# Post-norm transformer megakernel: layer norm scalings, the convolution's product groups and the sign FFN's routing stacks issued in another order

## The chip, the cores and the metric

The kernel runs on one core of one Trainium2 chip, as one program. The metric is the device time of that core in microseconds (us), taken as the median of several runs. The engines meant below are TensorE (PE: matmuls and transposes), VectorE (DVE), ScalarE (ACT), GpSimd (POOL) and SyncE (SP, which issues nearly all DMA transfers from one queue, in order).

## The reference

The input x is 2 batches x 1024 tokens x 1024 features, float32. Eight sublayers follow one another, each as `x = layernorm(x + f(x))`, in which the layer norm has no weights:

```python
x = ln(x + L0_attn(x))   # 8 heads of width 16, softmax over 1024 keys
x = ln(x + L0_ffn(x))    # t = x[:, perm]; 16 blocks 64 -> 256, gelu, -> 64; out[:, argsort(perm)]
x = ln(x + L1_attn(x))   # 3-tap convolution 1024 -> 768 over the tokens, gives q, k, v;
                         # causal attention inside blocks of 128 tokens; two projections
x = ln(x + L1_ffn(x))    # routing = softmax(x @ gate.T)                 (8 experts)
                         # (x * (routing @ in_scale)) @ sign(W).T * (routing @ out_scale) + bias
x = ln(x + L2_attn(x))   # Mamba block: selective scan, 2048 channels, 16 states
x = ln(x + L2_ffn(x))    # x[:, perm] @ dequantized int4 weights
x = ln(x + L3_attn(x))   # one-head attention
x = ln(x + L3_ffn(x))    # dense layer + 8 LoRA experts mixed by a router
```

(Here `L0_attn` has 8 heads over 128 columns, 16 each; its softmax is divided by sqrt(128).) The change touches layer 0, the convolution of `L1_attn` and the start of `L1_ffn`.

## The kernel before

The batches are worked one after the other, batch 1 about 2688 us behind batch 0, with the same code. The residual stream of a batch stays in SBUF twice: `x`, eight tiles of 128 tokens x 1024 features, and `xT`, its transpose, features on the partitions, in eight chunks of 128 features. Half h of a batch is tokens 512h to 512h + 511: tiles 0 to 3 or 4 to 7.

*Layer norm.* After each sublayer a tile goes through four steps. Its result is added into `x` out of PSUM, half a row at a time (`add_x`, L152, DVE), and its statistics are taken (`ln_stats`, DVE). `ln_roots` makes the reciprocal roots of several tiles at once (two small activations on ACT, five small steps on DVE). `ln_scale` (L185 to 187) is one DVE instruction of 128 x 1024 that subtracts the mean and multiplies by the root. `to_xT` (L126 to 135) transposes the tile on PE, eight transposes into two PSUM banks (L130), and copies each bank into `xT`; these copies alternate between DVE (L97) and ACT (L99). `add_y` (L139 to 148) is the first two steps for a tile that arrives transposed: eight transposes of `y` pieces, two additions, statistics.

*Order.* There are two ways. Inside `with self.tc.manual_schedule()` every engine executes its instructions in the order in which the Python text issues them. Outside of it a scheduler chooses. All lines of the change stand inside such blocks, though the code right behind the convolution's block is scheduled. Eight PSUM banks and eight 128 x 1024 weight buffers (`self.w`) go round; a load into a weight buffer waits until its last reader is done.

*Layer 0.* `attend(h)` works a half's attention in 16 steps, `blocks(h)` a half's FFN in eight steps j: `ups` (L424, PE) for the next j, Gelu on ACT, `downs` (PE), a copy `o` on DVE, and a scatter by POOL that undoes the permutation in DRAM (`yd`). `store(h)` writes `xT` of a half to DRAM (SP), `gather` reads it permuted (POOL, `t` pieces), and `back` reads `yd` again (SP, `y` pieces). The layer norm of one half is woven into the steps of another: `line(h, first, n)` builds a table `e` from step to work; `n[0]` to `n[3]` are the steps at which the four tiles get their sum and statistics (`first`), `n[4]` the step of the roots, `n[5:]` the steps of the four tiles' scaling and transposes. It is used three times: for tiles 0 to 3 within `attend(1)`, for tiles 4 to 7 within `blocks(0)`, and for tiles 0 to 3, with the FFN's result, within `blocks(1)`:

```python
e = line(0, project, (0, 1, 3, 4, 5, 6, 7, 8, 9))       # in attend(1)
e = line(1, project, (-1, -1, 0, 0, 1, 1, 2, 2, 3))     # in blocks(0); store(1) at 3
e = line(0, lambda tt: self.add_y(tt, ys), (2, 3, 3, 4, 5, 6, 6, 7, 7))  # in blocks(1)
```

*Layer 1's convolution.* The three taps are computed as a fast FIR scheme: `conv(h, co)` is one group of 128 output columns for a half, 32 matmuls of 256 tokens in four parts j of eight (L606), whose moving data are sums and differences of neighbouring tokens. For half 0 `sums0(j)` makes them on DVE. For half 1 POOL makes them (L573) in place, in `xT` itself and in `u0`, once tiles 4 to 7 are there. `calls(c, j)` issues one part of eight matmuls. `c0`, `c1` and `c2` are the first three groups of half 0. While c0 and c1 run, tiles 4 to 7 are still in layer 0's last layer norm (`add_y` to `to_xT`), and the two are interleaved by hand. In batch 0 the weights' sums are made by DVE (L593 to 595) and kept in DRAM for batch 1, and `l2_dequant`, called once per group from c2 on, unpacks a later sublayer's int4 weights: loads on SP, steps on DVE, scatters by POOL (L1516, L1519).

*Layer 1's sign FFN.* `route(h)` gives three steps: `logits` (PE, then ACT), `softmax` (DVE mostly), and `back`, whose last step writes `rT`, the transposed routing. `stack(out, in_, c)` splits a 32-row table into two parts of lower precision, stacked (one copy on ACT, two steps on DVE, the last at L912). It uses the small table `part`, loaded from DRAM at the start of the stage, and makes `ic` (input scales), `oc` (output scales) and `rT`. `signs(k)` turns one of eight weight chunks (`l_fw`, by SP) into signs on ACT. `scale(h, ks)` multiplies chunks of `xT` by `ic` x `rT` (PE L952, then DVE). `scale_in(tt)` splits a tile of `xT` into two parts `hi` and `lo` (ACT, DVE), `scale_out(tt)` makes the output scales (PE L967, ACT). `product(tt, nh)` is the matmul of a tile and half the columns. `project(tt, nh)`, from the stage before, is the last projection of convolution attention for tiles 4 to 7; its additions into `x` and statistics are DVE's.

Of the kernel before, what the change touches and what calls it, by code (L numbers as in the profile page):

```python
# [27 lines left out]
class Net:  # L28
# [185 lines left out]
    def l0(self, b):  # L214
# [7 lines left out]
        with self.tc.tile_pool(name=self.nm("l0a"), bufs=1) as lp, self.tc.tile_pool(name=self.nm("l0b"), bufs=2) as tp:  # L222
# [249 lines left out]
            def line(th, first, n):  # L472


                t4 = [4 * th + q for q in range(4)]
                e = {}
                for tt, m in zip(t4, n[:4]):
                    e.setdefault(m, []).append(lambda tt=tt: first(tt))
                e.setdefault(n[4], []).append(lambda: self.ln_roots(t4))
                for tt, m in zip(t4, n[5:]):  # L480
                    e.setdefault(m, []).append(lambda tt=tt: (self.ln_scale(tt), self.to_xT(tt)))
                return e

            def at(extra, n, f):
# [3 lines left out]
            with self.tc.manual_schedule():  # L488
                self.table()
                for s in (1, 0):  # L490
                    for _ in qkv(s, 0, False):
                        pass
                for tt in range(4, NT):
                    self.to_xT(tt)
                for _ in qkv(1, 1, False):
                    pass
                side = [f for s, th in ((0, 1), (2, 0), (2, 1)) for f in [qkv(s, th, True)] for _ in range(5 if s else 4)]
                for n, _ in enumerate(maxima(0)):
                    for f in side[:1]:
                        next(f)  # L500
                        del side[0]
                for f in side:
                    next(f)
                for tt in range(4, NT):
                    self.add_row(row, tt)
                m = maxima(1)
                attend(0, {n: [lambda: next(m)] for n in range(16)})
                e = line(0, project, (0, 1, 3, 4, 5, 6, 7, 8, 9))
                at(e, 9, lambda: store(0))
                at(e, 9, lambda: gather(0))  # L510
                attend(1, e)
                project(4)
                project(5)
                e = line(1, project, (-1, -1, 0, 0, 1, 1, 2, 2, 3))
                del e[-1]
                at(e, 3, lambda: store(1))
                for n in (5, 6):
                    at(e, n, lambda: gather(1, 2))
                at(e, 7, lambda: gather(1, 4))
                blocks(0, e)  # L520
                ys = back(0)
                e = line(0, lambda tt: self.add_y(tt, ys), (2, 3, 3, 4, 5, 6, 6, 7, 7))
                blocks(1, e)
# [6 lines left out]
    def l1_attn(self, b, yd, op):  # L530
        nc, i = self.nc, self.i
        row = self.row("l1_projb")
        with self.tc.tile_pool(name=self.nm("l1a"), bufs=1) as lp, self.tc.tile_pool(name=self.nm("l1s"), bufs=2) as spool:
# [105 lines left out]
            with self.tc.manual_schedule():  # L639
                c0[0]()  # L640
                sums0(0)
                sums0(1)
                c1[0]()
                ys = [t for q in range(4) for t in (vh[:, q, :HALF], vh[:, q, HALF:])]
                for k, t in enumerate(ys):
                    nc.sync.dma_start(t, yd[k * P : (k + 1) * P, :])

                def calls(c, j):
                    for f in c[1][8 * j : 8 * j + 8]:
                        f()  # L650

                calls(c0, 0)
                sums0(2)
                calls(c0, 1)
                calls(c0, 2)
                calls(c1, 0)
                self.table()
                self.add_y(4, ys)
                self.add_y(5, ys)
                self.ln_roots([4, 5])  # L660
                self.ln_scale(4)
                self.add_y(6, ys)
                self.to_xT(4)
                self.ln_scale(5)
                sums0(3)
                calls(c1, 1)
                self.to_xT(5)
                calls(c0, 3)
                c0[2]()
                c2 = conv(0, 2)  # L670
                c2[0]()
                self.add_y(7, ys)
                self.ln_roots([6, 7])
                calls(c1, 2)
                self.ln_scale(6)
                self.to_xT(6)
                self.ln_scale(7)
                calls(c1, 3)
                self.to_xT(7)
                c1[2]()  # L680
            for k in range(KD):
                sums(nc.gpsimd, 1, slice(k, k + 1), [(j, moving(1, j, k).unsqueeze(1)) for j in (2, 3, 0, 1)])
            for co in range(2, 6):
# [207 lines left out]
    def l1_ffn(self, b, project, early):  # L891
        nc, i = self.nc, self.i
        row = self.row("l1_fb")
        with self.tc.tile_pool(name=self.nm("l1f"), bufs=1) as lp, self.tc.tile_pool(name=self.nm("l1t"), bufs=2) as tp:
# [89 lines left out]
            with self.tc.manual_schedule():  # L984
                self.table()
                r0, r1 = route(0), route(1)
                r0[0]()
                project(4, 0)
                project(4, 1)
                r0[1]()  # L990
                project(5, 0)
                r0[2]()
                stack(ic, ics, 2)
                for k in range(KD):
                    signs(k)
                project(5, 1)
                scale(0, range(KD))
                stack(oc, ocs, 2)
                scale_in(0)
                scale_out(0)  # L1000
                project(6, 0)
                project(6, 1)
                self.table()
                project(7, 0)
                project(7, 1)
                self.ln_roots([4, 5, 6, 7])
                self.add_row(row, 0)
                for n in range(NT):
# [935 lines left out]
```

## Time and profile before

| | |
|---|---|
| time before, median of 3 runs | 5376.52 us (5371.23 to 5391.84) |
| profiled execution | 5374.18 us, its span 5372.4 us |
| mean granted TensorE clock | 0.964 of full speed |
| busy: PE / DVE / POOL / ACT | 92% / 60% / 38% / 36% of the span |

The stages that the change touches, in the trace of that execution (in us; batch 0 and batch 1):

| stage | length | PE busy | clock |
|---|---|---|---|
| layer 0, `attend(1)` | 58.0; 55 | 52.77; 49.78 | 0.94; 1.00 |
| layer 0, `blocks(0)` | 51.7; 52.4 | 40.83; 40.58 | 0.96; 0.96 |
| layer 0, `blocks(1)` | 53.0; 52.3 | 42.67; 42.16 | 0.94; 0.93 |
| convolution up to c2 | 52.7; 45.9 | 40.44; 38.30 | 0.87; 0.93 |
| convolution, the next groups | 69.7; 55.4 | 58.09; 55.40 | 0.93; 1.00 |
| sign FFN, logits to first product | 35.7; 35.0 | 23.81; 21.63 | 0.76; 0.80 |

The granted clock is the share of its full speed at which TensorE was let run. A row of the timeline reads: start, length, engine, source line, operation, output <- inputs, shape, and in brackets how long the engine had stood idle before it and what released it; so "[1.95 <-DVE x L186]" is 1.95 us of idle PE, ended by the DVE instruction of line 186 that writes `x`. A row of the waits reads: engine, what it wanted to do, what it waited for, then the total, the number of times and the longest. A row of the windows gives a stretch, its length, the busy time of PE, PE's weight loads, DVE, ACT and POOL (with the count of instructions), the granted clock, the DMA share and GB/s.

### The profile page before, as it was taken

How to read it: one execution, taken by the hardware profiler on the slowest of the kernel's cores; microseconds unless marked ns; L12 is line 12 of the kernel's file. 1: busy time of each engine (PE TensorE's matmuls, PEld its weight loads, DVE VectorE, ACT ScalarE, POOL GpSimd, SP SyncE). 2: the span in 40 equal slices, each digit the busy share in tenths (PEclk: the TensorE clock that was granted, in tenths of full speed). 3: DMA queues.
4: the chain of work that ended last, by engine and by line, in shares of the span. 5: the costliest groups of instructions: out<-in, count | busy, mean ns of one | idle time of the engine just before them, and what ended most of it. 6: DMA issues, size and time to landing. Idle time of an engine off the chain costs nothing.

```text
span 5372.4 us, 51914 instructions
## 1 busy us (share of the span) xinstructions
PE 4953.8 (92%) x17608; PEld 2461.5 (46%) x17608; DVE 3202.9 (60%) x4386; ACT 1944.0 (36%) x3935; POOL 2023.6 (38%) x1195
## 2 busy tenths in 40 slices
PE   8879988999999999998998899789999999999988
PEld 3346745444444444454433476454444444444533
DVE  5453256279999997314364422551899999953243
ACT  2421232367756552001024211323677665410110
POOL 1013110077778884100010220200877888821010
PEclk9999989999999999999999999899999999999989
DMA  2145311277787996101121432113877889950100
GB/s 92 40 149 180 100 50 50 97 225 210 209 243 213 262 265 196 63 32 43 47 72 40 145 121 90 53 53 104 243 206 214 244 225 262 262 170 32 63 8 32
DMA packets 263356, 726.00 MB, mean 135 GB/s; under 512 B 37040, under 2 KB 54576, under 8 KB 263092
## 3 DMA queue, kind: packets, MB, share of 16 engines
q1 hardware_dynamic: 256820, 701.70, 43.5%
q0 software_dynamic: 6272, 20.98, 1.1%
q8 instruction: 141, 2.31, 0.2%
q14 instruction: 123, 1.01, 0.1%
HBM read 617.43 MB, written 103.02 MB: 134 GB/s over the span
## 4 chain that ended last, share of the span: by engine, by line
PE 68%; DVE 13%; ACT 4%; DMA 3%; issue 2%; POOL 1%; SPq 0%; DVEq 0%; ACTq 0%; POOLq 0%
PE ps L104 26%; PE ps L1364 7%; PE ps L1254 6%; PE ps L606 5%; PE ps L1283 4%; PE ps L1579 4%; DVE h L1261 4%; PE ps L1403 3%; DVE h L1272 2%; PE ps L130 2%; PE ps L1317 2%; ACT ps L1256 1%; DVE st L163 1%; DMA h<-dxd 1%; DVE x L186 1%
## 5 line engine op out<-in xcount | busy, mean ns | idle before, releaser
L1246 POOL TENSOR_TENSOR h<-h,br 128x1024 f32<-128x1024 f32 x512 | 1204.1, 2373 | 28.6 <-DMA h<-dxd 17.9
L1256 ACT ACTIVATE ps<-ps,l_Alog 128x512 f32<-128x512 f32 x1024 | 669.0, 660 | 686.7 <-PE ps L1254 678.9
L1254 PE MATMUL ps<-hi,rep 128*128 128x512 f32 x1024 | 757.9, 740 | 23.3 <-DVE h L1261 14.9
L1261 DVE TENSOR_TENSOR_SCAN h<-ps,h 128x512 f32<-128x512 f32 x512 | 604.7, 1208 | 159.4 <-ACT ps L1256 159.4
L1261 DVE TENSOR_TENSOR_SCAN h<-ps,hst,h 128x512 f32<-128x512 f32 x512 | 632.5, 1266 | 16.0 <-ACT ps L1256 15.5
L1272 DVE TENSOR_TENSOR h<-h,ps 128x1024 f32<-128x1024 f32 x512 | 610.4, 1192 | 0.0
L104 PE MATMUL ps<-w,xT 128*128 128x512 f32 (+1 forms) x1280 | 520.8, 564 | 0.0
L1364 PE MATMUL ps<-xT,w 128*128 128x512 f32 x1024 | 516.4, 608 | 0.0
L1283 PE MATMUL ps<-h,sel 128*32 128x512 f32 x2048 | 410.1, 615 | 72.6 <-DVE h L1272 72.2
L1565 POOL TENSOR_TENSOR x<-x,row 128x1024 f32<-128x1024 f32 x48 | 112.6, 2345 | 876.7 <-PE ps L130 876.7
L152 DVE TENSOR_TENSOR x<-x,ps 128x512 f32<-128x512 f32 x192 | 128.9, 681 | 526.2 <-PE ps L104 379.2
L1254 PE MATMUL ps<-lo,rep 128*128 128x512 f32 x1024 | 408.8, 399 | 0.0
L104 PEld LDWEIGHTS ps<-w,xT 128*128 128x128 f32 x1280 | 248.0, 195 | 257.1 <-issue 250.2
L1254 PEld LDWEIGHTS ps<-hi,rep 128*128 128x128 f32 x1024 | 196.5, 192 | 350.0 <-issue 239.5
L104 PE MATMUL ps<-xT,w 128*128 128x512 f32 x768 | 336.8, 594 | 0.0
L177 ACT ACTIVATE rs<-mv 128x1 f32<-128x1 f32 (+2 forms) x88 | 17.9, 203 | 767.1 <-DVE mv L171 766.8
L130 PE MATMUL ps<-ident,x 128*128 128x128 f32 x1024 | 152.7, 301 | 148.5 <-DVE x L186 138.4
L1254 PEld LDWEIGHTS ps<-lo,rep 128*128 128x128 f32 x1024 | 196.3, 192 | 200.1 <-issue 195.3
L1212 POOL TENSOR_TENSOR e<-e,one 128x512 f32<-128x512 f32 x64 | 81.6, 1274 | 547.7 <-ACT one L1209 375.8
L1364 PEld LDWEIGHTS ps<-xT,w 128*128 128x128 f32 x1024 | 189.2, 192 | 175.3 <-issue 149.9
L1403 PE MATMUL ps<-w,w 128*128 128x512 f32 x512 | 268.0, 605 | 0.0
L1317 PE MATMUL ps<-xT,w 128*128 128x512 f32 x512 | 266.1, 605 | 2.0 <-DVE h L1261 1.9
(283 smaller groups left out, 7402.2 us busy)
## 6 DMA issues: line engine op xcount, KB each, us to landing
h<-dxd SPq DMA_DIRECT2D x512, 512.0 KB, 6.4
w<-l_in SPq DMA_DIRECT2D x128, 512.0 KB, 5.8
w<-l_out SPq DMA_DIRECT2D x96, 512.0 KB, 5.9
w<-l_conv SPq DMA_DIRECT2D x54, 512.0 KB, 3.5
w<-cvd SPq DMA_DIRECT2D x36, 512.0 KB, 3.2
w<-l_fw SPq DMA_DIRECT2D x32, 512.0 KB, 5.7
xcd<-xo SPq DMA_DIRECT2D x64, 256.0 KB, 2.1
szd<-zo SPq DMA_DIRECT2D x64, 256.0 KB, 3.7
```

The costliest lines, as they stand in the source:

```text
L104: self.nc.tensor.matmul(out, lhsT, rhs, start=j == 0, stop=j == n - 1)
L130: nc.tensor.transpose(p[:, j * P : (j + 1) * P], self.x[:, tt, k * P : (k + 1) * P], self.ident)
L606: nc.tensor.matmul(w["p", j // 2][:, 256 * (j % 2) : 256 * (j % 2) + 256], w["w"][j][:, k * P : (k + 1) * P], moving(th, j, k), start=k == ...
L1246: nc.gpsimd.tensor_tensor(hs[k], hs[k], norms[of(k)[0]][1].unsqueeze(1).to_broadcast([P, 2, HALF]), ALU.mult)
L1254: nc.tensor.matmul(dA[k, m], rep[:, 8 * jj + 4 * m + q, :], hl[u, c][n], start=n == 0, stop=n == 1)
L1256: nc.scalar.activation(dA[k, m], dA[k, m], AF.Exp, scale=A[:, g : g + 1])
L1261: nc.vector.tensor_tensor_scan(hs[k][:, m, :], dA.pop((k, m)), hs[k][:, m, :], hst[:, g : g + 1] if u else 0.0, ALU.mult, ALU.add)
L1272: nc.vector.tensor_tensor(hs[k], hs[k], norms[of(k)[0]][3].unsqueeze(1).to_broadcast([P, 2, HALF]), ALU.mult)
L1283: nc.tensor.matmul(py[u, c][32 * j : 32 * j + 32, :], self.sel[:, q, :], hs[k - 1 + j // 2][:, j % 2, :], start=False, stop=q == 3,)
L1317: nc.tensor.matmul(p, w["w"][:, k * P : (k + 1) * P], self.xcols(k, u0, HALF), start=k == 0, stop=k == KD - 1)
L1364: nc.tensor.matmul(p, w["w"][:, k * P : (k + 1) * P], self.xcols(k, u * HALF, HALF), start=k == 0, stop=k == KD - 1)
L1403: nc.tensor.matmul(p, y[:, cc, t * P : (t + 1) * P], wt[:, cc * HALF : (cc + 1) * HALF], start=c2 == 0 and cc == 0, stop=last,)
```

## The change

Only the order of issue changes.

1. In `line` the scalings of all four tiles are issued with the roots, at step `n[4]`; the steps `n[5:]` hold the transposes only. In `blocks(0)` the roots stay at step 1, and the transposes of tiles 4 to 7 move from steps 1, 2, 2, 3 to 2, 2, 3, 3. The store stays at step 3.
2. In the convolution, both scalings of tiles 4 and 5 follow their roots, and tiles 6 and 7 are added, rooted and scaled together before the last part of c0. The groups of eight matmuls now stand before and between the transposes of tiles 4 and 5, and c1's last part before those of 6 and 7.
3. In the sign FFN, the stack of `ic` follows the logits and the stack of `oc` the softmax. The last projections of tiles 6 and 7 stand between the scalings of `xT`, and `scale_in(0)` and `scale_out(0)` around the last ones.

```diff
@@ -477,8 +477,10 @@
                 for tt, m in zip(t4, n[:4]):
                     e.setdefault(m, []).append(lambda tt=tt: first(tt))
                 e.setdefault(n[4], []).append(lambda: self.ln_roots(t4))
+                for tt in t4:
+                    e[n[4]].append(lambda tt=tt: self.ln_scale(tt))
                 for tt, m in zip(t4, n[5:]):
-                    e.setdefault(m, []).append(lambda tt=tt: (self.ln_scale(tt), self.to_xT(tt)))
+                    e.setdefault(m, []).append(lambda tt=tt: self.to_xT(tt))
                 return e
 
             def at(extra, n, f):
@@ -511,7 +513,7 @@
                 attend(1, e)
                 project(4)
                 project(5)
-                e = line(1, project, (-1, -1, 0, 0, 1, 1, 2, 2, 3))
+                e = line(1, project, (-1, -1, 0, 0, 1, 2, 2, 3, 3))
                 del e[-1]
                 at(e, 3, lambda: store(1))
                 for n in (5, 6):
@@ -659,25 +661,25 @@
                 self.add_y(5, ys)
                 self.ln_roots([4, 5])
                 self.ln_scale(4)
+                self.ln_scale(5)
+                calls(c1, 1)
+                self.to_xT(4)
+                calls(c1, 2)
+                self.to_xT(5)
+                sums0(3)
                 self.add_y(6, ys)
-                self.to_xT(4)
-                self.ln_scale(5)
-                sums0(3)
-                calls(c1, 1)
-                self.to_xT(5)
+                self.add_y(7, ys)
+                self.ln_roots([6, 7])
+                self.ln_scale(6)
+                self.ln_scale(7)
                 calls(c0, 3)
                 c0[2]()
                 c2 = conv(0, 2)
                 c2[0]()
-                self.add_y(7, ys)
-                self.ln_roots([6, 7])
-                calls(c1, 2)
-                self.ln_scale(6)
+                calls(c1, 3)
+                c1[2]()
                 self.to_xT(6)
-                self.ln_scale(7)
-                calls(c1, 3)
                 self.to_xT(7)
-                c1[2]()
             for k in range(KD):
                 sums(nc.gpsimd, 1, slice(k, k + 1), [(j, moving(1, j, k).unsqueeze(1)) for j in (2, 3, 0, 1)])
             for co in range(2, 6):
@@ -985,24 +987,25 @@
                 self.table()
                 r0, r1 = route(0), route(1)
                 r0[0]()
+                stack(ic, ics, 2)
                 project(4, 0)
                 project(4, 1)
                 r0[1]()
+                stack(oc, ocs, 2)
                 project(5, 0)
                 r0[2]()
-                stack(ic, ics, 2)
                 for k in range(KD):
                     signs(k)
                 project(5, 1)
-                scale(0, range(KD))
-                stack(oc, ocs, 2)
+                project(6, 0)
+                scale(0, range(4))
+                project(6, 1)
+                scale(0, range(4, KD))
+                project(7, 0)
                 scale_in(0)
+                self.table()
+                project(7, 1)
                 scale_out(0)
-                project(6, 0)
-                project(6, 1)
-                self.table()
-                project(7, 0)
-                project(7, 1)
                 self.ln_roots([4, 5, 6, 7])
                 self.add_row(row, 0)
                 for n in range(NT):
```

## The prediction

> **What bounds the kernel now.** I read four views: the page's busy shares and the chain that ended last, then PE's waits in the windows of the three edited stages, then the timeline of PE there, and last the windows with the granted clock.
>
> ```profile
> PE 4953.8 (92%) x17608; PEld 2461.5 (46%) x17608; DVE 3202.9 (60%) x4386; ACT 1944.0 (36%) x3935; POOL 2023.6 (38%) x1195
> ...
> PE 68%; DVE 13%; ACT 4%; DMA 3%; issue 2%; POOL 1%; SPq 0%; DVEq 0%; ACTq 0%; POOLq 0%
> ```
>
> TensorE is the bound, and the 13% of DVE in the chain is where PE stands and waits for it. PE's waits, first 250 to 372 us (layer 0's FFN of batch 0), then 364 to 460 (the convolution), then 767 to 812 (sign FFN's start); columns are us in total, times, longest:
>
> ```profile
> PE ps L130 <- DVE x L186: 12.8, 8, 3.1
> ...
> PE ps L606 <- DVE w L594: 11.6, 2, 9.3
> PE ps L130 <- DVE x L186: 11.1, 2, 5.6
> ...
> PE ps L967 <- DVE oc L912: 7.1, 1, 7.1
> PE ps L952 <- DVE ic L912: 2.9, 1, 2.9
> ```
>
> L130 is a transpose of x, L186 the scaling in front of it, L912 the last step of a stack. All three edits aim at waits that are really there. The timeline of PE in batch 1 shows each:
>
> ```profile
> 2901.99 1.06 PE L130 MATMUL ps<-ident,x 128*128 128x128 f32 x8 [1.95 <-DVE x L186]
> ...
> 2951.65 1.21 PE L130 MATMUL ps<-ident,x 128*128 128x128 f32 x8 [3.06 <-DVE x L186]
> 2952.79 3.51 PE L424 MATMUL ps<-t,w 64*128 64x512 f32 x8
> ...
> 3024.38 1.09 PE L130 MATMUL ps<-ident,x 128*128 128x128 f32 x8 [1.54 <-DVE x L186]
> ...
> 3058.53 1.94 PE L130 MATMUL ps<-ident,x 128*128 128x128 f32 x8 [5.62 <-DVE x L186]
> ...
> 3456.43 1.22 PE L967 MATMUL ps<-oc,rT 32*128 32x512 f32 x2 [8.55 <-DVE oc L912]
> ```
>
> **The change, part by part.** It adds and removes no instruction of weight; it moves them. Durations: scaling 0.81 us, 0.73 more for each that follows directly; xT copy 0.69 on DVE, 0.59 on ACT; transposes of a tile 1.0; ups or downs 1.92; a group of eight products (L606) 3.47; eviction into x 0.69, statistics 1.5, roots 1.45.
>
> *Layer 0, attention of the second half.* Tile 2's scaling stands on DVE behind the evictions of the first heads, and PE waits 1.95 us in both batches. Scaled at step 5 it is long done. The price is three scalings (2.2 us) ahead of tile 0's xT copy, which comes 0.5 us later (rs ready 201.6 + 3.0 = 204.6, not 204.07); the exponentials pace PE there, so I take 0, at most 0.5. Gain 1.9.
>
> *Layer 0, first FFN half (batch 1's clock).* PE waits 3.06 + 1.61 + 1.16 + 1.61 = 7.4, and the L424 row takes 3.51 in place of 1.99, because Gelu's table load stood behind the xT copy: 9.0 together. With transposes from j=2 on, PE goes on at 2948.6: ups and downs end at 2952.4, the scalings run 2950.8 to 2953.8 beside them, tiles 4 and 5 follow without a wait, tiles 6 and 7 end at 2960.4 instead of 2969.5. What they delay is the o copy, by 1.4 us; its scatter has slack. The store on SP moves from 2969.8 to 2961.0. Next late is POOL: the gathers start when the store has landed, some 9.5 us on (2970.5), so they stay 8.8 ahead. I take 8.7.
>
> *Layer 0, second FFN half.* Waits 1.54 + 1.16 + 1.54 + 1.16 = 5.4. Scalings end at 3024.2, tile 3's transposes at 3028.9 instead of 3034.4. Next late is the last scatter: o is copied at 3026.9 instead of 3029.6, and the new pool's buffers are free 3.3 us after that scatter's start (3030.6 to 3033.9 today), at 3031.2. The sums that start the convolution move from 3034.8 to 3031.3. Gain 3.5, not 5.4. Layer 0 in all: 14.1 a batch, 28.2.
>
> *Convolution, batch 1.* Between 3050.1 and 3082.1 PE waits 5.62 + 1.94 and runs partly at half clock. New order: tiles 4 and 5's transposes to 3052.1, a group of products to 3055.5, a wait of 3.0 for the unchanged scaling at 3058.4, then transposes, group, transposes to 3063.8, y transposes to 3065.7, two groups to 3072.7. DVE meanwhile: scalings to 3059.1, two copies and u, sums0(3) to 3066.4, tiles 6 and 7 to 3071.8, roots and scalings to 3074.8. PE waits 1.5 and ends at 3075.9. Gain 6.2; PE is full from there to 3137, so it stays.
>
> *Convolution, batch 0.* PE reaches group 2 at 392.9 instead of 402.25, but DVE (w L593 to L595) and the queues take some back. The order of the built program shows on POOL that the first dequant scatter, today ahead of the 32 sums, now comes behind them:
>
> ```profile
> 398.77 0.98 POOL L1516 DMA_INDIRECT wq<-w,idx  x1 [50.88 <-DVE w L1515]
> 402.96 3.30 POOL L573 TENSOR_TENSOR xT<-xT 128x256 f32<-128x256 f32 x4 [3.20 <-DVE xT L97]
> 406.23 1.17 POOL L573 TENSOR_TENSOR u<-xT 128x256 f32<-128x256 f32 x2
> 407.36 17.78 POOL L573 TENSOR_TENSOR xT<-xT 128x256 f32<-128x256 f32 x26
> 425.29 0.98 POOL L1516 DMA_INDIRECT wq<-w,idx  x1 [0.15 <-issue]
> ```
>
> On SP the second l_packed load now waits for that scatter, and the next l_conv loads are queued behind it. The sums can start at 391.5 (ACT's copies) and end near 413.5. Then: scatter lands +3.3, l_packed +3.9, DVE 1.5, l_conv +3.9, L593 and L594 2.5: group 4 starts near 430 to 432, today at 439.3; group 5 near 451, today 457.9. Between 3 and 9 gained; I take 7, from the last.
>
> *Sign FFN.* The in-stack's DVE step now stands at the head of the queue and waits for l_part; behind it are tile 4's evictions, which release the logits' softmax. l_part is issued at 768.10, and DMA is idle from 770.5 on, so it costs no more than that. Then DVE is the bound without a gap: stack to 772.5, evictions and statistics to 775.3, softmax 1.9, out-stack 2.0, eviction 0.7, rT 1.5, three evictions with two statistics 4.9, eight scalings of xT 4.8, eviction 0.7, lo 1.3, eviction and statistics 2.1, roots 1.45, lo 1.3, scaling 0.7: 798.7. Tile 4's transposes follow at 799.1, today at 809.22: 10.1. Signs are covered: the fifth l_fw load waits for the in-stack alone (771 instead of 780.8), the sixth for the out-stack (778), so they end near 789, before hi is wanted. PE's projections (3.5 us a tile) are spread over DVE's 24 us. In batch 1 l_part lands 1.4 us later after the logits: 9.5. Together 19.6.
>
> **The clock.** Rows: the same wait of 1.95 us, in batch 0 and in batch 1.
>
> ```profile
> 211.80:214.30 2.50, 0.63 (x8) 0.39 (x4) 1.70 (x4) 0.00 (x0) 0.00 (x0) 1.00 0.00 0
> ...
> 216.00:218.00 2.00, 2.00 (x8) 1.27 (x7) 0.46 (x1) 2.00 (x5) 0.00 (x0) 0.50 0.00 0
> ...
> 2902.00:2904.00 2.00, 2.00 (x13) 1.67 (x14) 1.34 (x2) 0.91 (x2) 0.00 (x0) 1.00 0.04 8
> ```
>
> The Trainium skill ("TensorE: Matmul & The Clock Gate", part 1, "What's actually happening") halves the clock only after an idle window of about 3.4 us. By that rule the gaps left in the new order (3.1, 1.5, 2.8, 1.9 us a batch) cost nothing. The row disagrees: a 1.95 us wait was followed by some 6 us at 0.50. By the row each gap may bring a spell of 3 to 6 us at half speed, 1.5 to 3 us lost, in half of the cases: up to 12 in all. I take 3, since today's gaps, which go, had such spells too.
>
> **Sum.** 28.2 + 6.2 + 7 + 19.6 - 3 = 58. The profiled execution took 5374.2 (span 5372.4 and 1.8 around it), so 5316; the median of the runs shown, 5376.5, lies 2.3 above it: 5318. A difference of 0.5% (27 us) is about what a measurement of this kernel can tell from no change; it took 5371 to 5392 in three runs.
>
> **Rivals.**
> Half of it lost (12%): gaps re-throttle PE again and again (12) and batch 0's convolution gives nothing (7), layer 0's gathers or y loads land late and keep a third of its gain (9): 58 - 25 = 33, 5344. For: y loads already hold PE at 2997 to 3002. Against: store, gathers and y loads all move together.
> No change (8%): layer 0's transfers keep all 24 us of its two FFN halves, and DVE, which is gapless in sign FFN, keeps half of 20: 58 - 34 - 7 = 17 left, 5360. Against: waits for DMA are 3 us there, those for L186 are 13.
> Slower (4%): SP in batch 0's convolution. Each group from the third on, and the projections behind them, then waits in turn for scatter, l_packed, DVE and l_conv, about 16 us by my sum against 14 of products. The slowest landings in the trace (7.2 for l_conv there, not 3.9) would add 3 to each of four rounds. It turns the result only if a round takes 15 us longer than I reckon, four times 15 = 60: 5380, and past 22 it is over 0.5%, 5405. Nothing in the trace is so slow.
> That the scheduler undoes the order is excluded: the built program has the instructions of PE, DVE and ACT as the text of the change puts them.
>
> **The numbers.** My own case has 76%. The range reaches down to 5300: clock spells gone (3), batch 0's own spell of 6 us at half clock gone too (3), its convolution at 9 (2), layer 0's second FFN half at the full 5.4 (4), and the fastest run, 5 below the median, come to 17. Up it reaches to 5346, past the first rival. Faster by over 0.5% takes my case and most of the first rival: 0.86; within 0.5%: 0.10; slower: 0.04.
>
> **What would show it.** Right: no L130 waits for L186 in layer 0's FFN; first sums of the convolution 14 us earlier in each batch; 46 us from there to group 2 becoming 40 in batch 1; logits to tile 4's transposes 32 us instead of 42. Wrong: PE waits of over 2 us for t, y or l_conv in their place, a first dequant scatter later than 16 us before group 4, or a mean clock below 0.964.

## The result, and the profile after

The changed kernel takes 5320.76 us (median of 4 runs, 5318.64 to 5322.97) against 5373.88 us before (4 runs, 5364.95 to 5391.84): a ratio of 0.9897, 95% interval 0.9871 to 0.9923. The profiled execution took 5320.85 us, with a span of 5318.8 us and a mean granted clock of 0.968.

The page's line of busy shares, as before:

```profile
PE 4939.3 (93%) x17608; PEld 2457.1 (46%) x17608; DVE 3195.9 (60%) x4386; ACT 1943.6 (37%) x3935; POOL 2030.5 (38%) x1195
```

TensorE was busy for 4953.8 us before, in the same 17608 matmuls. 14.5 us of the 53.6 that the span lost are therefore matmuls that ran at a better clock (over the whole span the time at half clock fell from 386 to 341 us), and the rest is idle time.

PE's waits in the three edited stages of batch 0: layer 0's FFN (238 to 322 us), the convolution (322 to 453), sign FFN's start (747 to 792). Columns: us in total, times, longest. From the convolution on, line numbers are two higher than before: L608 is the product that was L606, L575 the sums (L573), L595 to L597 the weights' sums (L593 to L595); behind the sign FFN they are three higher (L1519 was L1516).

```profile
PE ps L393 <- DVE aoT L390: 3.1, 2, 2.4
PE ps L424 <- DVE o L450: 1.5, 1, 1.5
...
PE ps L608 <- DVE w L596: 19.5, 4, 10.7
PE ps L608 <- DVE qh L575: 8.2, 1, 8.2
PE ps L130 <- DVE x L186: 4.6, 2, 3.0
...
PE ps L943 <- DVE r L938: 3.0, 1, 3.0
PE ps L130 <- DVE x L186: 1.6, 1, 1.6
```

Layer 0's waits for L186 are gone (12.8 us before, in the view shown with the prediction), and so are sign FFN's waits for the stacks. The convolution is where the time did not go away. Its waits for the scaling fell from 11.1 us to 4.6, but those for groups' weights rose from 11.6 to 19.5 (the longest, group 4's, was there before with 9.3), and ahead of its first product PE now waits 8.2 us for the first sum (L575), where it waited 1.8.

The stages, from the start of one named instruction to the start of another, in us. In brackets is the time at half clock in the stage, taken from the trace's clock records; it agrees with what the windows view gives as 2 x (1 - granted clock) x length.

| stage | batch 0, before | after | batch 1, before | after |
|---|---|---|---|---|
| second half's attention, to the first `ups` | 65.9 (9.4) | 61.1 (2.5) | 64.9 (6.3) | 61.2 (2.7) |
| `blocks(0)` | 51.7 (4.3) | 42.1 (0.9) | 52.5 (3.9) | 43.0 (0.7) |
| `blocks(1)`, to the first product | 53.0 (6.8) | 48.7 (4.5) | 52.3 (6.8) | 48.6 (9.0) |
| convolution, to the projections | 122.2 (23.9) | 123.5 (22.8) | 101.1 (6.8) | 99.0 (8.1) |
| sign FFN, logits to first product | 35.7 (17.1) | 24.8 (3.4) | 35.1 (13.7) | 24.6 (3.4) |
| sign FFN, first product to last addition | 102.6 (13.7) | 106.6 (20.5) | 102.7 (13.7) | 103.5 (13.7) |

The sum of the gains: layer 0 18.7 and 16.9, convolution -1.3 and 2.1, sign FFN's start 10.9 and 10.5, its products -4.0 and -0.8. That is 53.0 of 53.6; all other stages together give the remaining 0.6, with parts of both signs (the scan of batch 1 alone took some 8 longer, that of batch 0 some 3 less).

### The profile page after: what moved, and what is told of

Same layout as the page of the kernel before. It is cut to its first block, busy times and chain, and to the rows that moved or that the text cites. A ratio compares the mean times of both kernels' runs of the same rounds, so it can differ in the third digit from the quotient of the medians.

```text
span 5318.8 us, 51900 instructions
## 1 busy us (share of the span) xinstructions
PE 4939.3 (93%) x17608; PEld 2457.1 (46%) x17608; DVE 3195.9 (60%) x4386; ACT 1943.6 (37%) x3935; POOL 2030.5 (38%) x1195
## 5 line engine op out<-in xcount | busy, mean ns | idle before, releaser
L1249 POOL TENSOR_TENSOR h<-h,br 128x1024 f32<-128x1024 f32 x512 | 1204.8, 2376 | 24.8 <-DMA h<-dxd 13.3
L1264 DVE TENSOR_TENSOR_SCAN h<-ps,hst,h 128x512 f32<-128x512 f32 x512 | 633.3, 1269 | 14.5 <-ACT ps L1259 14.2
L1118 DVE SCALAR_TENSOR_TENSOR ps<-xp,l_convw,ps 128x512 f32<-128x512 f32 x192 | 144.5, 753 | 185.8 <-ACT ps L1113 181.2
```

What stands on the lines that cost most here:

```text
L1118: nc.vector.scalar_tensor_tensor(p, xp[:, k : k + HALF], cw[:, c, k : k + 1], p, ALU.mult, ALU.add)
L1249: nc.gpsimd.tensor_tensor(hs[k], hs[k], norms[of(k)[0]][1].unsqueeze(1).to_broadcast([P, 2, HALF]), ALU.mult)
L1264: nc.vector.tensor_tensor_scan(hs[k][:, m, :], dA.pop((k, m)), hs[k][:, m, :], hst[:, g : g + 1] if u else 0.0, ALU.mult, ALU.add)
```

## The experiments

Each was timed against the kernel before on the same chip. Where an expectation speaks of "the changed kernel", its time is the 5320.76 above; it was not timed again beside the later versions. The kernel before came out between 5372.95 and 5377.84 in these series, so a difference of less than about 5 us between two versions' medians says little by itself.

**Each part alone.** The first is `line` with its changed call, the second the convolution's block, the third sign FFN's block; the rest of each is the kernel before.

> The kernel before with part 1 alone (scalings behind their roots in line, transposes of tiles 4 to 7 at steps 2, 2, 3, 3). Theory A (the gain is the sum of its stages, each keeping what its own trace shows): layer 0 gained 18.7 us in batch 0 and 16.8 in batch 1 of the changed kernel, so 32 to 36 us faster than before, about 5340. Theory B (layer 0's gain is partly eaten at the handover to the convolution, where the last scatter sets the start, and the changed convolution wins some of it back only together with it): under 28 us, 5347 or more. Theory C (most of the gain is TensorE's clock that happens to fall better): no relation to 35; anything from 10 to 50.

> The kernel before with part 2 alone (the convolution's groups and layer norms of tiles 4 to 7). In the changed kernel this stage, from its first product to the attention projections behind it, went from 122.2 to 123.5 us in batch 0 and from 101.2 to 99.0 in batch 1. Theory A: this part is worth 1 to 4 us in all, within 0.1% of before. Theory B (it lost its gain because layer 0 now ends earlier than its last scatter, so that TensorE stands 8.2 and 4.7 us ahead of the first product and works the first group at half clock, 9.96 and 9.46 us for 7.14): without part 1 the first group is at full clock, batch 1 gains 5 to 6 and batch 0 gains 2 to 7, together 7 to 13 us faster. Where batch 0 gains nothing even so, it is the dequantization's scatters behind the sums on GpSimd.

> The kernel before with part 3 alone (sign FFN's stacks under the logits). Theory A: from logits to the first product 10.5 to 10.9 us a batch less, all of it kept: 21 us faster, about 5353. Theory B (batch 0 of the changed kernel gave 3.9 us back between the first and the last product; the new order brings that back with it): 10.5 + 7 = 17 us, 5357. Theory C: the batch that gave back did so by two half-clock spells that come and go with the phase of the clock's windows, so this run can show 14 to 21.

| part alone | median, us | ratio to before, 95% | gain of its stages in the trace, batch 0 and 1 |
|---|---|---|---|
| layer 0 | 5340.9 (6 runs) | 0.9942, 0.9926 to 0.9957 | 14.9, 13.8 |
| convolution | 5371.5 (14 runs) | 1.0000, 0.9989 to 1.0012 | 2.2, 4.5 |
| sign FFN, to the first product | 5360.1 (20 runs) | 0.9970, 0.9961 to 0.9980 | 10.9, 10.9 |

The ratios give 31, 0 and 16 us, together 47 of the 55 that the ratio of all three gives; the intervals are 5 to 8 us to either side, so the parts are additive as far as these runs can tell. Layer 0 is worth most, and as much as theory A said. (The execution that was profiled for it was the slowest of its six, 5360.9 us at a clock of 0.962, so its stages show rather too little.) Part 3 came out nearer to theory B's 17 us than to A's 21, and by the medians at 13: what it gains at its start it lost in part again behind it, as in batch 1, where the products took 104.9 us with 17.1 us at half clock, against 102.7 with 13.7 before. That fits theory C's mechanism.

Part 2 alone fits theory A by its time: the interval, 6 us to either side of no change, leaves out theory B's 7 to 13. Its trace lies between the two, since the stages gained 6.7 us there and other stages gave some of it back. In batch 1 the first group now runs at full clock (7.14 us, where it takes 9.46 in the changed kernel) and the stage takes 96.6 us; so the handover from layer 0 did eat part of that gain (theory B). In batch 0 it gains 2.2 us only. PE's waits there, in the timeline (a group is a row of `qh` and one of `kh`; these are the first halves of groups 3, 4 and 5):

```profile
407.64 10.01 PE L606 MATMUL ps<-qh,w 128*128 128x256 f32 x32 [3.75 <-DVE w L594]
433.88 8.85 PE L606 MATMUL ps<-qh,w 128*128 128x256 f32 x32 [9.32 <-DVE w L594]
452.81 7.17 PE L606 MATMUL ps<-qh,w 128*128 128x256 f32 x32 [3.17 <-DVE w L594]
```

The wait of 9.3 us for group 4's weights stays even without part 1, as it stood in the kernel before, so layer 0 is not its cause.

**Layer 0 without the shift of the transposes.**

```diff
-                e = line(1, project, (-1, -1, 0, 0, 1, 2, 2, 3, 3))
+                e = line(1, project, (-1, -1, 0, 0, 1, 1, 2, 2, 3))
```

> The changed kernel, but in blocks(0) the transposes of tiles 4 to 7 stay at steps 1, 2, 2, 3, as before; the scalings still follow their roots. Theory A (the scalings' place does it): the transposes of tile 4 wait some 3 to 4 us behind the roots of step 1 again, the other three wait for nothing: 3 to 5 us a batch slower than the changed kernel, 6 to 10 in all. Rival (the shift does most of it, as TensorE has nothing else to do beside the roots at step 1): 12 us or more slower, with the long L424 row (3.51 us) back.

5330.50 us (6 runs, ratio 0.9924, 0.9908 to 0.9941): 10 us slower than the changed kernel. `blocks(0)` takes 49.5 and 48.7 us instead of 42.1 and 43.0, and PE waits there once for L186:

```profile
PE ps L130 <- DVE x L186: 3.1, 1, 3.1
```

The scalings' new place removes three of the four waits. The first one, in front of tile 4, is as long as before, since nothing else stands between the roots and that tile's transposes. In the traces the shift is worth 7.4 and 5.7 us of the 9.6 and 9.5 that `blocks(0)` gained; part of it is the clock, for the wait comes with 8.4 and 4.4 us at half clock. That is more than theory A gave it (3 to 5 a batch), and 13 us together is what the rival had said, though the 10 by the medians is not. The rival's sign, the long L424 row, came back in batch 1:

```profile
2929.53 1.09 PE L130 MATMUL ps<-ident,x 128*128 128x128 f32 x8 [3.06 <-DVE x L186]
2930.56 3.68 PE L424 MATMUL ps<-t,w 64*128 64x512 f32 x8
```

In batch 0 it is 2.57. The row is long by as much of it as runs at half clock (2930.6 to 2934.0 in batch 1; in batch 0 only up to 1.2 us into the row).

**Weights ahead of the dequantization, and the dequantization behind all groups.**

```diff
+            nxt = c2
             for co in range(2, 6):
-                load, cs, last = conv(0, co) if co > 2 else c2
-                if co > 2:
-                    load()
+                load, cs, last = nxt
...
                 last()
+                if co < 5:
+                    nxt = conv(0, co + 1)
+                    nxt[0]()
                 if b == 0:
                     self.l2_dequant(co - 2)
```

> The changed kernel, but in the convolution's loop the next group's weights are asked for ahead of the dequantization of this group, so that on SP no l_conv load is queued behind an l_packed load that waits for a scatter. In the changed kernel groups 2 to 5 of batch 0 wait 1.8, 3.8, 10.7 and 3.2 us for the weights' sums, and group 4 also runs its first half at half clock; first product to projections takes 123.5 us. Theory A (the scatter behind GpSimd's sums holds the SP queue, and that is where batch 0's gain went): the wait of 10.7 falls to 2 or less, the stage to 110 to 114, batch 1 unchanged, 10 to 13 us faster than the changed kernel. Rival (the weights' sums on DVE and the DMA queues are the limit anyway): group 5 or the projections wait for what group 4 saves; the stage stays over 119, less than 4 us.

> The changed kernel, but all four dequantizations of batch 0 are issued behind the convolution's groups instead of one behind each. Theory A: as with the loads ahead, the convolution's stage of batch 0 falls from 123.5 to about 108 to 112 (no scatter, no l_packed ahead of any l_conv); the projections behind it then share SP and DVE with the dequantization, and the attention stage of batch 0 (294.5) grows by 0 to 10. Rival: the groups still wait for their weights' sums, as SP can load a group's 1.5 MB only when the group two before has ended: waits of 2 to 4 us a group stay, stage over 117.

With the loads ahead: 5308.51 us (5 runs, ratio 0.9874, 0.9858 to 0.9890), 12 us faster than the changed kernel. The timeline of PE, batch 0, groups 3 (second half) to 5 and the projections:

```profile
400.97 7.07 PE L608 MATMUL ps<-kh,w 128*128 128x256 f32 x32
408.55 7.14 PE L608 MATMUL ps<-qh,w 128*128 128x256 f32 x32 [0.51 <-DVE w L596]
415.53 7.07 PE L608 MATMUL ps<-kh,w 128*128 128x256 f32 x32
427.65 8.72 PE L608 MATMUL ps<-qh,w 128*128 128x256 f32 x32 [5.05 <-DVE w L596]
436.21 7.07 PE L608 MATMUL ps<-kh,w 128*128 128x256 f32 x32
443.35 1.10 PE L104 MATMUL ps<-qkv,w 128*128 128x512 f32 x2
447.97 2.93 PE L104 MATMUL ps<-qkv,w 128*128 128x512 f32 x3 [3.52 <-DMA w<-l_wq]
```

Group 4's wait of 10.7 us is 0.5, the stage takes 108.2 us instead of 123.5, and 5.3 us of that are lost again in the attention behind it (299.8 for 294.5), which waits for its own weights. Theory A holds: the SP queue, held by an l_packed load that waits for a scatter, was where batch 0's gain went.

With the dequantization behind all groups: 5314.89 us (5 runs, ratio 0.9884, 0.9868 to 0.9899), 6 us faster than the changed kernel. From group 2 to the projections there is no wait for weights at all, yet the stage takes 115.8 us, since PE then stands before the projections:

```profile
PE ps L104 <- DMA w<-l_wq: 14.9, 1, 14.9
```

The expected place was right and the size wrong: the whole dequantization moves in front of the next weights on SP, and 7.7 of the 12 to 15 us are left, of which attention takes another 3.6.

**TensorE kept busy ahead of the first product.**

```diff
+                p = self.ps()
+                for n in range((56, 32)[b]):
+                    nc.tensor.transpose(p[:, P * (n % 4) : P * (n % 4) + P], self.ident, self.ident)
                 calls(c0, 0)
```

> The changed kernel with 56 (batch 0) and 32 (batch 1) transposes of the identity added ahead of the convolution's first product; their results are read by nothing. TensorE stands there today for 8.2 and 4.7 us. Theory A (the clock is granted by how busy TensorE was in the window of 3.4 us before): the first group runs at full clock, 7.1 us instead of 9.96 and 9.46, and everything behind it comes 2.8 and 2.3 us earlier; the added work fits into the wait. 5 us faster in all. Rival (the half clock has another cause, or the added work is too late or too long): the first group still takes over 9 us, or it starts later by what it gains; 0 or slower.

5316.17 us (5 runs, ratio 0.9882, 0.9865 to 0.9899). The timeline of PE at batch 1's first product, L656 being the added transposes:

```profile
2991.39 3.66 PE L656 MATMUL ps<-ident 128*128 128x128 f32 x32
2996.26 7.14 PE L608 MATMUL ps<-qh,w 128*128 128x256 f32 x32 [1.21 <-issue]
```

The first group takes 7.14 us in both batches, and batch 1's stage takes 95.0 us with no time at half clock, 6.1 less than before the change, where the prediction had reckoned 6.2 at full clock. Of the 4.0 us against the changed kernel the first group is 2.3. The rest is not the added work's doing: the wait of 3.05 us ahead of tile 4's transposes is here too, and this time no half clock followed it. No other engine's work was moved, and the sums still come when they came. Batch 0 does not show it in the length of its stage (124.1), as its later groups wait for weights anyway. The 4.6 us by the medians are inside the intervals; the verdict rests on the rows.

**The last scatter's source outside layer 0's pool.** (The indices that it reads move too.)

```diff
+                    if th and j >= KD - 1:
+                        o = self.bp.tile([P, D], F, tag="row", name=self.nm("o"))[:, :HALF]
+                    else:
+                        o = tp.tile([P, HALF], F, tag="o", bufs=3, name=self.nm("o"))
```

> The changed kernel, but the copy that the last scatter of layer 0's FFN reads, and the table of indices, lie in a pool that outlives layer 0, so that the convolution's first sums need not wait until that scatter has landed. Theory A (the handover waits for the last scatter alone, which itself waits for the scatter before it): DVE's first sum comes 6.4 us (batch 0) and 3.0 us (batch 1) earlier, right behind the last copy into xT; TensorE's wait falls to 1.8 us, as in the kernel before, the first group runs at full clock (7.1 us); together 9 to 14 us faster than the changed kernel. Rival (the y pieces for tiles 4 to 7 are next late, since they can be read only when the scatter has landed): the first group comes earlier but TensorE then waits at L144 for vh by the same amount; under 5 us.

5313.07 us (5 runs, 5297.46 to 5321.72; ratio 0.9876, 0.9856 to 0.9895). By its time it lies between the theories, 8 us faster than the changed kernel. Batch 1 does what theory A says: `blocks(1)` to the first product takes 43.4 us instead of 48.6. In batch 0 it takes 46.2 instead of 48.7, and PE then waits at a new place. (In this kernel L612 is the product, L579 the sums, L600 the weights' sums.)

```profile
PE ps L612 <- DVE w L600: 19.9, 4, 11.2
PE ps L130 <- DVE x L186: 4.6, 2, 3.0
PE ps L612 <- DVE kh L579: 4.4, 1, 4.4
PE ps L612 <- DVE cb L563: 1.8, 1, 1.8
```

A sum (kh) stands on DVE behind the weights' sums of group 1. Their third load had fallen behind the row l1_bv on SP, which waits for the very scatter that was to be taken out of the way. The stage grew by 5.0 us. For batch 0 that is the rival's outcome by another road, a weight load and not the y pieces.

**Both, and with more waits filled.** The first mends that load's place. The second adds `self.fill(n)`, n transposes of the identity, ahead of four waiting instructions.

> The changed kernel with the loads ahead of the dequantization and the last scatter's source outside layer 0's pool, and the row l1_bv (which waits for that scatter when it takes the source's place) loaded behind the convolution's first weights, so that the third l_conv load of group 1 is no longer queued behind it on SP. Theory A (two separate waits, so their gains add): the convolution's stage of batch 0 at 108 to 111, layer 0's second FFN half to the first product at 45 to 46 in batch 0 and 43 to 44 in batch 1, attention of batch 0 some 5 longer; 15 to 20 us faster than the changed kernel, 5300 to 5306. Rival (with the first group earlier, the weight loads and the y pieces take it back as they did in batch 0 of the kernel with the last scatter's source alone, whose stage grew by 5): no faster than the kernel with the loads ahead alone, 5308.

> The same with transposes of the identity that nothing reads put into four waits of TensorE: 12 ahead of tile 4's transposes in the convolution (a wait of 3.05 us), 12 ahead of sign FFN's first routing transposes (2.96), 28 ahead of the second half's logits (4.2) and 36 ahead of its first scaling (5.4); some 0.11 us each, so that 1.1 to 1.7 us of each wait are left. Theory A (a wait halves the clock of the next window or two of 3.4 us when it leaves TensorE idle for more than about 1.75 us of a window): the half-clock spells behind these waits go, and with them 13.7 to 20.5 us at half clock per batch in the sign FFN's products become 7 or less; 6 to 12 us faster than the kernel of the run before. Rival (the granted clock follows something slower than one window, or the added work delays the waiting work itself): the spells stay, within 3 us of the run before, or slower.

5307.68 us (4 runs, 5298.67 to 5313.93; ratio 0.9871, 0.9851 to 0.9891) and 5303.15 us (4 runs, 5293.92 to 5303.45; 0.9863, 0.9845 to 0.9881). The first is no faster than the loads ahead alone: in batch 0 convolution and attention take 414.3 us instead of 408.0, as group 5 now waits 8.2 us for its weights, and batch 1's `blocks(1)` to the first product takes 47.0 us with 6.8 at half clock, not 43.4. The gains do not add (the rival). The second shows its effect in sign FFN's products of batch 1; these are two windows, of the kernel without and of the kernel with filled waits (columns: window, length, busy PE, weight loads, DVE, ACT, POOL, granted clock, DMA share, GB/s):

```profile
3399.60:3504.50 104.90, 87.28 (x383) 64.31 (x382) 72.92 (x150) 27.85 (x62) 10.37 (x6) 0.92 0.08 28
...
3392.80:3493.80 101.00, 88.84 (x447) 68.51 (x446) 74.25 (x153) 28.37 (x62) 10.42 (x6) 0.98 0.09 29
```

PE does more work there in less time: the half-clock time falls from 17.1 to 3.4 us (in batch 0 from 17.1 to 6.8) and the stage by 3.9. Between the two kernels' medians lie 4.5 us, less than the expected 6 to 12 and inside the intervals.

**Loads ahead, and waits filled.**

> The changed kernel with the loads ahead of the dequantization, with the waits filled as in the run before, and with 56 and 30 transposes of the identity ahead of the convolution's first product in place of the moved source of the last scatter. The moved source gained 5 us at the handover of batch 0 and lost them in that batch's convolution and attention (408 us with the loads ahead alone, 414 with both), and gained up to 5 in batch 1. Theory A (full clock behind the filled waits is worth what the clock table says, and the weights of batch 0 stay in time): batch 0's convolution and attention at 405 to 408, batch 1's convolution at 94 to 96, the products of the sign FFN at 101 to 103 in both batches; 8 to 12 us faster than with the loads ahead alone: 5296 to 5300. Rival (TensorE's time saved there is waited for again): 5303 or more.

5295.86 us (4 runs, 5289.41 to 5301.60; ratio 0.9852, 0.9832 to 0.9871): 25 us faster than the changed kernel and 13 faster than the loads ahead alone by the medians, and the fastest version that was run. Batch 0's convolution and attention take 403.9 us, batch 1's convolution 96.7, the products 99.5 and 101.1. The profiled execution's clock is 0.975.

## Why the prediction was right, point by point

The forecast was 5318 and the measurement 5320.76. The mechanism was right in layer 0 and sign FFN; that the sum came out within 3 us is luck in part. Two terms were wrong in opposite directions: layer 0 gave 7 us more than forecast and the convolution 12 less. The forecast also started from a median of 5376.5, which a fourth run brought to 5373.9: the gain was 53 us, not 58.

| term | predicted | in the trace |
|---|---|---|
| second half's attention, twice | 3.8 | 8.5 |
| first FFN half, twice | 17.4 | 19.1 |
| second FFN half, twice | 7.0 | 8.0 |
| convolution, batch 1 | 6.2 | 2.1 |
| convolution, batch 0 | 7 | -1.3 |
| sign FFN, logits to tile 4's transposes | 19.6 | 20.2 |
| clock, and what lies behind | -3 | -3.0 (remainder) |

- *Clock.* The last row agrees by chance. The -3 stood for half-clock spells behind the gaps that are left, but in the trace each stage's figure holds its own spells already, and the -3.0 is what the other rows leave of 53.6, mostly the products (-4.8). What the clock did shows in PE's busy time: 14.5 us less for the same matmuls. The term had the wrong sign.
- *Sign FFN.* From logits to tile 4's transposes it takes 31.5 us in batch 0 and 31.6 in batch 1, for 42.0 and 41.4 before: 10.4 and 9.8, forecast 10.1 and 9.5. DVE is the bound there, as the step said: in batch 0, from the landing of l_part (751.8 us) to tile 4's transposes (779.2), it waits 0.8 us in all. The order that reads worst, a step waiting for l_part at the head of the queue, cost next to nothing, since the projection that DVE takes next came out of PE no earlier than about 751.4 (half of a row of 3.70 us that starts at 749.57).
- *Layer 0.* The waits went as listed. The excess of 7.4 us over 28.2 is mostly clock: in the stretch of the second half's attention the time at half clock fell by 6.9 and 3.6 us, worth half of that each. Where it did not fall, the stretch gained what was forecast: in the kernel with the added transposes, batch 0 had 10.2 us at half clock there (9.4 before) and took 63.4 us, 2.5 less than before for a forecast of 1.9. The prediction had booked such spells as a loss and set the ones that go against the ones that come; they should have been counted stage by stage. One reading was wrong too, without harm to the sum: the L424 row of 3.51 us was put down to Gelu's table load. This window of the kernel before lies over it; PE is busy throughout, at half clock:

```profile
2952.49:2955.90 3.41, 3.41 (x11) 1.20 (x9) 0.54 (x1) 2.88 (x4) 0.00 (x0) 0.50 0.00 0
```

  The wait of 3.06 us ahead of the row left PE idle for 2.57 us of the window before this one, so wait and long row went together.
- *The last scatter.* It did set the start of the convolution, as the step for the second FFN half said. What was not seen: o was ready 1.2 us (batch 1) and 4.8 us (batch 0) before its scatter started, since each scatter waits for the one before it to land (figures in the last section). Because layer 0's work now ends well ahead of it, PE stands idle for 8.2 and 4.7 us before the first product and runs the first group at half clock. That makes 2.3 of the 4.1 us that batch 1's convolution fell short of its 6.2; another 1.4 went to the group behind the wait of 3.05 us, which takes 4.98 us instead of 3.62.
- *Convolution, batch 0.* This is the step that failed. Its chain was right: first dequantization scatter, l_packed, DVE, l_conv, sums, group 4. It puts 16.5 to 18.5 us from the end of GpSimd's sums to group 4, and the trace has 18.8 (401.2 to 420.0). (Its terms add up to 15.1; the slack above them covered l_conv, which took 7.3 us from its first issue to the sum that waits for it, not 3.9.) The term that was mis-sized is the sums' own time, taken from the row before as 22 us. They took 26.4:

```profile
374.82 6.94 POOL L575 TENSOR_TENSOR xT<-xT 128x256 f32<-128x256 f32 x9 [45.15 <-ACT xT L99]
...
383.42 17.77 POOL L575 TENSOR_TENSOR xT<-xT 128x256 f32<-128x256 f32 x20
401.34 1.00 POOL L1519 DMA_INDIRECT wq<-w,idx  x1
```

  The sums also started 3.1 us later than reckoned, most of it the 2.8 us of the half-clock first group. Together that is 7.5 us, and the forecast was a gain of 7. Why the sums took longer stands in the last section: the new order puts them beside other steps of DVE. The kernel with the loads ahead tests the queue: without l_conv queued behind that scatter the stage falls by 15.3 us, though the sums take 26.1 there. The share of the 7.5 us is read from rows of a trace; no run changed the sums' time alone.
- *The rivals.* "Half of it lost" named its parts rightly (batch 0's convolution gives nothing, PE slows again behind its gaps) but not their balance, since layer 0 did not lose a third. The rival that ends slower named the right place, the rounds on SP in batch 0; they cost 8 us against the forecast, not 60. "No change" did not come: layer 0's two FFN halves gave 27 us, where that rival had their transfers keep all 24.
- *The signs to look for.* "No L130 waits for L186 in layer 0's FFN" and "32 us instead of 42" came true. The first sums came 18.7 and 16.8 us earlier, counted from the second half's attention, where 14 was said. "46 us becoming 40 in batch 1" did not: it is 45.2, from 47.3, measured from the first sum. Of the signs of a wrong forecast one showed: a wait of over 2 us for l_conv's sums in the old one's place.

## What to carry to other kernels

When a step is moved up, ask which instruction now stands in front of an in-order queue with a wait that used to be satisfied: here it was one scatter behind 32 sums, and by way of SP and DVE it cost a stage its whole gain. Do not take an instruction's duration from a row in which another engine did other work beside it. A gap on TensorE costs its own length and the slow time behind it, so reckon a stage with both, and where a gap can't be removed, work that nothing reads can fill it.

## What the runs showed of the hardware

**The clock is decided window by window.** In the trace's clock records every change of the granted clock lies on one grid, and spells last 3.41 us or a multiple of it. That explains why the same wait of 1.95 us in layer 0 was followed by half clock in batch 0 and not in batch 1. These are windows cut on that grid, of the kernel before, first around the wait of batch 0 (212.4 to 214.4 us), then around that of batch 1 (2900.0 to 2902.0); the second column is the length and the third TensorE's busy time, the clock stands behind the five engines:

```profile
211.58:214.99 3.41, 1.46 (x14) 1.06 (x11) 1.70 (x4) 0.00 (x0) 0.00 (x0) 1.00 0.00 0
214.99:218.41 3.42, 3.42 (x13) 1.96 (x10) 1.41 (x2) 2.56 (x5) 0.00 (x0) 0.50 0.00 0
218.41:221.82 3.41, 3.41 (x15) 1.23 (x14) 0.00 (x0) 0.00 (x0) 0.00 (x0) 0.50 0.00 0
...
2897.88:2901.29 3.41, 2.16 (x15) 0.58 (x12) 1.15 (x4) 1.10 (x3) 0.00 (x0) 1.00 0.00 0
2901.29:2904.70 3.41, 2.71 (x15) 2.02 (x16) 1.97 (x3) 1.61 (x4) 0.00 (x0) 1.00 0.02 5
```

In batch 0 the whole wait fell into one window (1.46 us busy, 1.95 idle); in batch 1 it was split (1.25 and 0.70 idle). Counted over both traces, before and after, of the full-clock windows that left TensorE idle for 2.0 us or more all 109 were followed by a window at half clock; of those with less than 1.5 us idle 7 of 2741 were; in between it was 17 of 61. So a wait of 2 us may be free or may cost 1.7 to 3.4 us more (half of a spell of 3.41 or 6.83), by where it falls on the grid. This bears out the row that the prediction sided with, and it agrees with the added transposes: in both batches the first group behind them ran at full clock. Runs of one kernel lie up to 35 us apart (33 runs of the kernel before: 5358.49 to 5393.01), and the longer ones have the lower clock: the ten at a mean clock of 0.963 or less average 5381.8 us, the ten at 0.966 or more 5366.1. That the grid makes this difference is likely, and was not tested.

**GpSimd's sums slow down beside some of DVE's steps, not all.** One sum of 128 x 256 takes 0.61 us, and up to 1.64 when it meets a DVE instruction that reads two tiles from SBUF, such as the weights' sums or the dequantization's last step (`w<-w,w`, 128 x 1024), which then takes up to 1.52 us itself, and 1.23 without a sum beside it. From the changed kernel, batch 0:

```profile
390.78 1.23 DVE L595 TENSOR_TENSOR w<-w,w 128x1024 f32<-128x1024 f32 x1
390.83 1.64 POOL L575 TENSOR_TENSOR xT<-xT 128x256 f32<-128x256 f32 x1
392.04 1.52 DVE L596 TENSOR_TENSOR w<-w,w 128x1024 f32<-128x1024 f32 x1
```

In all 13 traces every sum longer than 1.3 us overlaps such an instruction for 1.0 us or more, and no sum of 0.6 us does; beside DVE steps that read from PSUM the sums keep their time (7 to 9 such sums in each of five traces, 0.605 to 0.622 us). Batch 1 has no such meeting, and the 32 sums take 18.2 to 18.3 us in every trace. Batch 0 has four in the three kernels without part 2 (22.2 us), and seven or eight in the ten with it (26.1 to 26.4). So the longer time could have been counted: about 1 us for each meeting. In nine of these ten, two more sums took 0.93 to 1.09 us beside a one-input step of the dequantization; how that comes is open.

**Scatters into one tensor follow one another.** In the changed kernel the last two of layer 0's FFN scatters start 3.4 us apart in batch 1 (2978.18 and 2981.61), while the second one's data was ready at 2980.45. The DMA records show the first one's data moving until 2980.53. In batch 0 they start 6.1 us apart (319.12 and 325.19): the first one's data moved only from 322.4 to 323.9, beside a weight load of 524 KB (320.7 to 323.9).
